# Spacing GpSimd's indirect gathers over the slots of two pairs, and building the tokens' places in two steps, in a masked attention kernel

## The chip, the cores and the metric

The kernel runs on one core of one Trainium2 chip. The metric is the device time of one execution in microseconds (us). The core has five engines that each work through a queue of their own in program order: TensorE (PE), VectorE (DVE), ScalarE (ACT), GpSimd (POOL) and SyncE (SP); they wait for each other through semaphores only. DMA transfers are issued from the queues of SP and POOL (and of ACT at the very end).

## The reference

`x` is (8, 512, 1024) f32: 8 batches, 512 features, 1024 tokens. The mask `cond` is (8, 1024) of zeros and ones.

```python
xt = transpose(x, (0, 2, 1))
q = xt @ Wq.T                                    # 512 -> 512, 8 heads of 64
qh = q.reshape(B, T, 8, 64).transpose(0, 2, 1, 3)
scores = einsum('bhqd,bhkd->bhqk', qh, qh) / 8   # q = k = v
logits = (scores * cmask + (1 - cmask) * -1e30) * rmask
ctx = einsum('bhqk,bhkd->bhqd', softmax(logits), qh)
out = x + transpose(ctx.reshape(B, T, 512) @ Wo.T, (0, 2, 1))
```

About half the tokens are kept (mask 1). All dropped tokens of a batch have one and the same result, that of the mean of the values, so only the kept tokens and one mean row need attention.

## The kernel before, in words

**Tiles and loops.** For each batch the kept tokens are gathered into NK = 544 rows: four chunks of 128 and a last one of 32 (NC = 5 chunks). The work is a sequence of 32 pairs of heads, p = 0 to 31, four in each batch: pair (b, pr) is batch b and heads 2 pr and 2 pr + 1. Each pair is walked in five slots c = 0 to 4, one for each chunk. In a slot PE makes the scores `s` (L601), ACT their exponentials `e` (L605; `el` for the last, short chunk), and VectorE adds up the slot before (`add_up`, L622, two instructions). After the five slots `attend` multiplies exponentials and values (`av`, PE L638) and ACT copies the sums to `cT` (L654).

**Side work in the slots.** Each slot also carries pieces of other pairs and batches: projections `pq` (PE L529, copied by ACT to `qT`, L536), values `v` (PE L551, ACT L554), the squared lengths of the values and their largest (`sq` ACT L559, `len` and `top` DVE L561 and L568), which `bias_of` turns round on PE (`top`, L574) and makes into the maximum `m` and the exponentials' bias (DVE L576 to L579); the reciprocal sums, turned on DVE (`rt`, L708), spread by DMA (`rb`) and multiplied in by `contexts` (DVE L726 to L735).

**Tokens in and out.** `turn` transposes the next batch's x on VectorE (L417) and SP stores it to DRAM as rows `xd`. `search` (DVE L473, L476) finds which token goes to which row (`source`), and `gather` (POOL indirect DMA, L485) fetches those rows as `xin`, five gathers a batch. `put_mean` and `collect` (PE L512, L498) transpose them to `xc`. `output` (PE L750, ACT L757) makes a batch's finished rows, which POOL stores to DRAM as `od` (L759). `fetch` (POOL indirect DMA, L852) gathers them back in the order of all 1024 tokens, eight gathers `g_0` to `g_7` a batch, by the indices `block_origin`. `finish_blocks` (DVE transpose L819 and add L822) adds each `g` to x, and SP stores the sum.

**The places.** `block_origin` comes from `place_all`, which runs once, in batch 0 at pair 1, slot 4: five VectorE instructions make `home` (L1048 to L1052), PE transposes it (`home_t`, L1054), and two more VectorE instructions copy it to `placed` and `origin` (L1055, L1056). `place_blocks` (DVE L803, 16 casts) makes `block_origin` from `placed` at pair 2, slot 2.

**What sets the order.** Everything is written in the order in which each engine is to run it; nothing reorders it. The tables in `late` name the slots (pr, c) of the side work: `TURN`, `SEARCH` (`LATER` for batch 0) and `FINISH`. In a slot the order is scores, `add_up` of the slot before, contexts, turn, search, gather, loads, fetch, places, finish, then projections, bias, outputs, collects and values.

Of the kernel before, what the change touches and what calls it, by code (L numbers as in the profile page):

```python
# [10 lines left out]
F32 = mybir.dt.float32  # L11
# [294 lines left out]
def attention_of_kept_tokens(ctx, tc, x, mask, wq, wo, out, ident, wqT, woT, verdict, flag):  # L306


    nc = tc.nc
    B, D, T = x.shape  # L310
    P = 128
# [3 lines left out]
    NT = T // P  # L315
# [5 lines left out]
    NC = -(-LONG // P)  # L321
    LAST = NC - 1
# [6 lines left out]
    def fit_to(n):  # L329
        nonlocal NK, KH, END  # L330
        NK, KH, END = n, n // 2, n - LP
        assert DK % END == 0
        sizes[:] = [P] * LAST + [END]
        places[:] = [slice(END + c * P, END + (c + 1) * P) for c in range(LAST)] + [slice(0, END)]

    sb = ctx.enter_context(tc.tile_pool(name="fsb", bufs=2))
# [11 lines left out]
    block_origin = keep.tile([P, B, NT], I32, name="block_origin")  # L348
# [6 lines left out]
    homes = [keep.tile([B * NT, P], F32, name=f"home_{i}") for i in range(2)]  # L355
# [3 lines left out]
    def bank(name):  # L359
        return ps.tile([P, NB], F32, tag="t", name=name, bufs=4)  # L360
# [119 lines left out]
    def gather(b, i):  # L480
        n = sizes[i]
        if i == 0:
            xins[b] = []
        xin = sb.tile([P, D], F32, tag="xin", name=f"xin_{b}_{i}", bufs=NC)
        nc.gpsimd.indirect_dma_start(  # L485
            out=xin[:n, :],
            out_offset=None,
            in_=xds[b],
            in_offset=bass.IndirectOffsetOnAxis(ap=searches[b][2][:n, i : i + 1], axis=0),
        )  # L490
        xins[b].append(xin)
# [246 lines left out]
    ods, gs, xrs = {}, {}, {}  # L738
# [107 lines left out]
            )  # L846
            gs[b, i] = g

    def fetch(b):
        for i in range(NT):  # L850
            g = sb.tile([P, D], F32, tag="g", name=f"g_{b}_{i}", bufs=NT)
            nc.gpsimd.indirect_dma_start(  # L852
                out=g,
                out_offset=None,
                in_=ods[b],
                in_offset=bass.IndirectOffsetOnAxis(
                    ap=block_origin[:, b, i : i + 1], axis=0
                ),
            )
            gs[b, i] = g  # L860

    def finish_tokens(b, i):

# [50 lines left out]
    def load_weights(w, nm, queue=None):  # L914
        ws = []
        for e in range(ND):
            t = sb.tile([P, D], F32, tag="g", name=f"{nm}_{e}", bufs=NT)
            (queue or nc.sync).dma_start(t, w[e * P : (e + 1) * P, :])
            ws.append(t)
        return ws  # L920
# [122 lines left out]
    def place_all():  # L1043

        BC = B * NT
        mrow, rank = seen["mrow"], seen["rank"]
        home, wrap = homes
        nc.vector.tensor_scalar(home, rank, float(-NK), None, ALU.add)  # L1048
        nc.vector.tensor_tensor(home, home, mrow, ALU.mult)
        nc.vector.tensor_scalar(home, home, float(NK - 1 + END), None, ALU.add)  # L1050
        nc.vector.tensor_scalar(wrap, home, float(NK), float(-NK), ALU.is_ge, ALU.mult)
        nc.vector.tensor_tensor(home, home, wrap, ALU.add)  # L1052
        pt = bank("home_t")
        nc.tensor.transpose(pt[:, :BC], home, ident[:BC, :BC])  # L1054
        nc.vector.tensor_copy(placed, pt[:, :BC].rearrange("p (b c) -> p b c", c=NT))  # L1055
        nc.vector.tensor_copy(origin, placed)  # L1056

    def late(n):
        fit_to(n)
        weights["wq"] = order_columns(load_weights(wq, "wq"), "wq")  # L1060
        mean_of(0)
        for i in range(NC):
            gather(0, i)
        queries_of(0)
        load_batch(1, nc.gpsimd)
        load_ranks(1, nc.gpsimd)
        put_mean(0)
        for i in range(NC):
            collect(0, i)
            if i < ND:  # L1070
                turn_weights(wqT, "wq", i)
        weights["wo"] = load_weights(wo, "wo", nc.gpsimd)
        for hf in range(2):
            project(pairs[0], hf)
        values(pairs[0])
        project(pairs[1], 0)
        bias_of(pairs[0])


        TURN = [(0, 2), (0, 4), (1, 0), (1, 1)]  # L1080
        SEARCH = {(1, 0): (0, 1), (1, 1): (2,), (1, 2): (3,), (1, 3): (4,)}
        LATER = {(1, 1): (0,), (1, 2): (1,), (1, 3): (2, 3), (1, 4): (4,)}

        FINISH = {
            (2, 3): (0,),
            (2, 4): (1, 2),
            (3, 0): (3,),
            (3, 1): (4,),
            (3, 2): (5,),
            (3, 3): (6,),  # L1090
            (0, 1): (7,),
        }
        FINISH_LAST = {(3, 1): (0, 1), (3, 2): (2, 3), (3, 3): (4,)}
        for p, pair in enumerate(pairs):
            b, pr = pair
            before = pairs[p - 1] if p else None
            todo = slots_of(p)
            for c in range(NC):
                scores(pair, c)
                if c:  # L1100
                    add_up(pair, c - 1)
                if c == 0 and before:
                    add_up(before, LAST)
                    if p + 1 < len(pairs):
                        invert(before)
                    else:
                        inv = inverses(before)
                if p + 1 == len(pairs):
                    if c == 1:
                        spread(before, inv)  # L1110
                        contexts(before)
                elif c == (4, 2, 3, 4)[pr] and before:
                    contexts(before)
                if (p, c) in ((2, 3), (len(pairs) - 2, 1)):
                    bias_of(pairs[p + 1])
                if b + 1 < B:
                    if (pr, c) in TURN:
                        turn(b + 1, TURN.index((pr, c)))
                    if pr < 2 and pr * NC + c < NN * ND:
                        add_features(b + 1, pr * NC + c)  # L1120
                    if pr == 1 and c == 3:
                        mean_of(b + 1)
                    for i in (SEARCH if b else LATER).get((pr, c), ()):
                        search(b + 1, i)
                    if pr == 0 and c == 1:
                        queries_of(b + 1)
                    if pr == 1 and c == (3 if b else LAST):
                        for i in range(NC):
                            gather(b + 1, i)
                if pr == 3 and c == 0 and b + 2 < B:  # L1130
                    load_batch(b + 2)
                    load_ranks(b + 2)
                if pr == 1 and c == 2 and b > 0:
                    load_rest(b - 1)
                if pr == 2 and c == 0 and b > 0:
                    fetch(b - 1)
                if p == 1 and c == 4:
                    place_all()
                if p == 2 and c == 2:
                    place_blocks()  # L1140
                for i in (FINISH if b + 1 < B or pr == 0 else FINISH_LAST).get((pr, c), ()):
                    of = b - 2 if pr == 0 else b - 1
                    if of in BLOCKS:
                        finish_blocks(of, i)
                for task in todo[c]:
                    task()
                issue_stores()
            if p + 1 < len(pairs):
                attend(pair)
        last = pairs[-1]  # L1150
        add_up(last, LAST)
        attend_last(last)
        for i in (0, LAST, *range(1, LAST)):
            end_output(B - 1, i)
        for i in range(5, NT):
            finish_blocks(B - 2, i)
        issue_stores()
        worst = sb.tile([P, 2], F32, tag="worst", name="worst")
        nc.vector.tensor_reduce(
            worst[:, 0:1], low.rearrange("p h c -> p (h c)"), axis=AX.X, op=ALU.min  # L1160
        )
        nc.vector.tensor_reduce(worst[:, 1:2], lowest, axis=AX.X, op=ALU.min)
        nc.vector.tensor_tensor(worst[:, 0:1], worst[:, 0:1], worst[:, 1:2], ALU.min)
        pt = bank("worst_t")
        nc.tensor.transpose(pt[:1, :P], worst[:, 0:1], ident)
        one = sb.tile([1, 1], F32, tag="one", name="one")
        nc.vector.tensor_reduce(one, pt[:1, :P], axis=AX.X, op=ALU.min)
        nc.vector.tensor_scalar(one, one, TINY, None, ALU.is_lt)
        nc.vector.tensor_copy(flag, one)
        issue_stores()  # L1170
        fetch_last(B - 1)
        for i in range(NT):
            finish_tokens(B - 1, i)
# [96 lines left out]
```

## Time and profile before

| | |
|---|---|
| median of 3 runs | 774.1 us (770.66, 774.1 and 782.16) |
| profiled execution | 778.75 us, of which the span is 776.8 us and 1.95 us lie around it |
| mean granted clock of TensorE | 0.929 |
| busy in the span | PE 668.4 us (86%), DVE 533.5 (69%), ACT 378.6 (49%), POOL 171.4 (22%) |
| mean DMA rate | 150 GB/s |

Rows of the trace are read so: start and duration in us, engine, line, operation, out<-in, shape and count; in brackets the engine's idle time just before the row and what ended it. A row with x8 is eight like instructions joined. `PEclk` is the TensorE clock that was granted, as a share of full speed. In the rows below, pairs and slots are found by their time: pair 1 of batch 0 ends its last scores at 65.56 us, and batches 1 to 6 take the stretches from 141.30 to 676.70 us.

### The profile page before, as it was taken

Reading aid. Unit: us, or ns where it says so; the run is one execution under the profiler, and the core shown is the slowest. Engines: PE = TensorE matmul, PEld = TensorE weight load, DVE = VectorE, ACT = ScalarE, POOL = GpSimd, SP = SyncE. Lnnn points to the kernel's source line nnn. Section 1 sums busy time; section 2 is a strip of 40 time slices with the busy share of each in tenths; the row PEclk is TensorE's granted clock in tenths of the full one; section 3 lists DMA queues with packets and bytes.
Section 4 is the critical chain, followed back from the end, with each engine's and each line's share of the span. In section 5 each row is a group of like instructions: output and inputs, shape, how many; then the busy total and the mean of one; then the engine's idle time right before and its main releaser. Section 6 shows DMA issues by size and latency. Waiting matters only on the chain.

```text
span 776.8 us, 11988 instructions
## 1 busy us (share of the span) xinstructions
PE 668.4 (86%) x4139; PEld 387.6 (50%) x4139; DVE 533.5 (69%) x1568; ACT 378.6 (49%) x763; POOL 171.4 (22%) x222
## 2 busy tenths in 40 slices
PE   5795899978999599995999989997999599997972
PEld 4663565445555265553555555554554265553431
DVE  6178758736877389863898579866887389545762
ACT  5384567334664256534474546646574256434400
POOL 4702000070102501044010521035001600033030
PEclk9797999988999799996999999999999789998985
DMA  7534042771479605894248834895468700753247
GB/s 273 193 111 128 18 154 61 187 209 37 153 180 224 196 3 172 209 230 141 84 136 213 213 111 153 208 230 163 153 166 211 222 4 22 181 137 113 54 129 210
DMA packets 96703, 116.41 MB, mean 150 GB/s; under 512 B 10304, under 2 KB 74304, under 8 KB 96624
## 3 DMA queue, kind: packets, MB, share of 16 engines
q1 hardware_dynamic: 79552, 74.07, 36.2%
q0 software_dynamic: 12848, 39.30, 15.8%
q10 hardware_dynamic: 4224, 2.10, 0.9%
q8 instruction: 36, 0.59, 0.3%
q14 instruction: 43, 0.35, 0.2%
HBM read 72.78 MB, written 42.65 MB: 149 GB/s over the span
## 4 chain that ended last, share of the span: by engine, by line
PE 79%; ACT 7%; DVE 5%; issue 3%; another core or an unknown queue 2%; DMA 2%; POOL 1%; DVEq 0%; POOLq 0%
PE s L601 20%; PE av L638 18%; PE pq L529 16%; PE po L750 13%; ACT e L605 5%; PE xc L498 3%; PE v L551 2%; PE pa L770 2%; DVE junk L622 1%; DVE junk L473 1%; DMA g<-od,origin 1%; PE xt L393 1%; PE po L786 1%; PE mean L512 1%
## 5 line engine op out<-in xcount | busy, mean ns | idle before, releaser
L622 DVE CUSTOM_DVE_ANT_0 junk<-e,valid 128x544 f32<-128x544 f32 x256 | 185.1, 723 | 97.8 <-ACT e L605 79.6
L601 PE MATMUL s<-qT 64*128 64x272 f32 (+1 forms) x1280 | 190.6, 438 | 56.6 <-ACT e L605 44.8
L605 ACT ACTIVATE e<-s,bias 128x544 f32<-128x544 f32 x256 | 170.8, 712 | 64.2 <-PE s L601 33.8
L601 PEld LDWEIGHTS s<-qT 64*128 64x128 f32 (+1 forms) x1280 | 95.8, 182 | 141.3 <-ACT e L605 77.0
L529 PE MATMUL pq<-xc,wqT 128*128 128x272 f32 x512 | 136.4, 410 | 4.7 <-issue 3.7
L638 PE MATMUL av<-e,v 128*64 128x272 f32 x1024 | 130.2, 401 | 0.4
L529 PEld LDWEIGHTS pq<-xc,wqT 128*128 128x128 f32 x512 | 93.7, 193 | 40.1 <-issue 11.2
L750 PE MATMUL po<-woT,cT 128*128 128x512 f32 (+1 forms) x448 | 107.4, 436 | 0.0
L638 PEld LDWEIGHTS av<-e,v 128*64 128x64 f32 x1024 | 69.6, 138 | 51.6 <-ACT v L554 8.8
L759 POOL DMA_DIRECT2D od<-oc x56 | 29.9, 536 | 273.4 <-ACT oc L757 272.4
L750 PEld LDWEIGHTS po<-woT,cT 128*128 128x128 f32 (+1 forms) x448 | 47.1, 150 | 52.5 <-issue 51.3
L654 ACT COPY cT<-av 128x272 f32<-128x272 f32 x62 | 21.4, 388 | 101.2 <-PE av L638 79.9
L852 POOL DMA_INDIRECT g<-od,block_origin x56 | 57.3, 1022 | 18.9 <-issue 15.5
L757 ACT COPY oc<-po 128x512 f32<-128x512 f32 (+1 forms) x35 | 18.3, 522 | 81.4 <-PE po L750 81.4
L536 ACT COPY qT<-pq 128x272 f32<-128x272 f32 x64 | 24.7, 386 | 60.4 <-PE pq L529 57.2
L381 POOL TENSOR_SCALAR valid<-count,kept 128x544 f32<-128x544 f32 x8 | 13.5, 1693 | 177.4 <-DVE sums L622 177.3
L485 POOL DMA_INDIRECT xin<-xd,source x40 | 41.1, 1028 | 48.2 <-DVE bias L579 26.7
L561 DVE TENSOR_REDUCE len<-sq 128x10 f32<-128x640 f32 x32 | 25.8, 808 | 30.1 <-ACT sq L559 30.1
L417 DVE STREAM_TRANSPOSE xt<-x 128x1024 f32<-128x1024 f32 x28 | 34.7, 1240 | 13.6 <-DMA xd<-xt 13.5
L473 DVE TENSOR_SCALAR_CACHE_REDUCE junk<-rank,key 128x1024 f32<-128x1024 f32 (+4 forms) x40 | 39.7, 993 | 1.6 <-ACT rank L1020 1.6
L822 DVE TENSOR_TENSOR xr<-o,xr 128x512 f32<-128x512 f32 x56 | 38.8, 692 | 1.9
L819 DVE STREAM_TRANSPOSE o<-g 128x512 f32<-128x512 f32 x56 | 39.2, 701 | 0.0
(139 smaller groups left out, 638.5 us busy)
## 6 DMA issues: line engine op xcount, KB each, us to landing
x<-in_x_dram SPq DMA_DIRECT2D x56, 256.0 KB
xd<-xt SPq DMA_DIRECT2D x112, 128.0 KB
xr<-in_x_dram SPq DMA_DIRECT2D x28, 512.0 KB
out_dram<-xr SPq DMA_DIRECT2D x24, 512.0 KB
rb<-row SPq DMA_DIRECT2D x60, 160.0 KB
od<-oc POOLq DMA_DIRECT2D x28, 256.0 KB
rank<-ranks SPq DMA_DIRECT2D x6, 512.0 KB
xd<-xt POOLq DMA_DIRECT2D x8, 256.0 KB
```

Source lines behind the costliest of these rows:

```text
L417: nc.vector.transpose(xt.rearrange("p k (d f) -> p k d f", d=ND), xs[b][r][:, :, at : at + n].rearrange("p d (k t) -> p k d t", t=Q),)
L473: nc.vector.tensor_scalar(junk[:, :n], rank[:, i * P :], key[:, col], 0.0, ALU.is_le, ALU.add, accum_out=found[:, col])
L485: nc.gpsimd.indirect_dma_start(out=xin[:n, :], out_offset=None, in_=xds[b], in_offset=bass.IndirectOffsetOnAxis(ap=searches[b][2][:n, i : ...
L529: nc.tensor.matmul(pq[:, :KH], wqT[:, d, pr * P : (pr + 1) * P], xcs[b][:, d, cols], start=(d == 0), stop=(d == ND - 1),)
L601: nc.tensor.matmul(s[to, h, :KH], qT[heads[h], keys], qT[heads[h], queries], start=True, stop=True)
L605: nc.scalar.activation(e[:, hf if c < LAST else 0, :, :], s[:, :, :KH], AF.Exp, bias=biases[pair][:, c : c + 1], scale=SCALE,)
L622: nc.vector.tensor_tensor_reduce(junk[:, :n].rearrange("p (f k) -> p f k", k=KH), e[:, :, h, :], (valid if c < LAST else part).rearrange(" ...
L638: nc.tensor.matmul(av[head, :KH], v[keys, c, head], e[keys, hf if c < LAST else 0, h, :], start=(c == 0), stop=(c == LAST),)
L750: nc.tensor.matmul(po[k * n : (k + 1) * n, :w], cTs[b, pr][:, i * P : i * P + n], woT[:, pr, k * w : (k + 1) * w], start=(pr == 0), stop=( ...
L819: nc.vector.transpose(o.rearrange("p k t -> p (k t)"), gs[b, i])
L822: nc.vector.tensor_tensor(to, o, to, ALU.add)
L852: nc.gpsimd.indirect_dma_start(out=g, out_offset=None, in_=ods[b], in_offset=bass.IndirectOffsetOnAxis(ap=block_origin[:, b, i : i + 1], a ...
```

## The change

`fetch` now issues one gather, and a table `FETCH` calls it once in each of the slots (2, 0) to (2, 4) and (3, 0) to (3, 2). Before, all eight were issued at (2, 0). The five gathers of the next batch's tokens go by the tables `GATHER` and `GATHER_LATER` (batch 0); before, all five stood at (1, 3), in batch 0 at (1, 4). `FINISH` has one block in each slot from (2, 3) to (3, 4); before, (2, 4) had two and (3, 4) none. `place_all` is cut in two: the five VectorE instructions for `home` move to pair 0, slot 1, and the transposition with its two copies, now `turn_places`, stays at pair 1, slot 4.

```diff
-    def fetch(b):
-        for i in range(NT):
-            g = sb.tile([P, D], F32, tag="g", name=f"g_{b}_{i}", bufs=NT)
-            nc.gpsimd.indirect_dma_start(
...
+    def fetch(b, i):
+        g = sb.tile([P, D], F32, tag="g", name=f"g_{b}_{i}", bufs=NT)
+        nc.gpsimd.indirect_dma_start(
...
         nc.vector.tensor_tensor(home, home, wrap, ALU.add)
+
+    def turn_places():
+        BC = B * NT
         pt = bank("home_t")
-        nc.tensor.transpose(pt[:, :BC], home, ident[:BC, :BC])
+        nc.tensor.transpose(pt[:, :BC], homes[0], ident[:BC, :BC])
         nc.vector.tensor_copy(placed, pt[:, :BC].rearrange("p (b c) -> p b c", c=NT))
         nc.vector.tensor_copy(origin, placed)
...
+        GATHER = {(1, 3): (0, 1), (1, 4): (2, 3), (2, 0): (4,)}
+        GATHER_LATER = {(1, 4): (0, 1, 2), (2, 0): (3,), (2, 1): (4,)}
+        FETCH = {(2, k): (k,) for k in range(NC)} | {(3, k): (NC + k,) for k in range(NT - NC)}
         FINISH = {
             (2, 3): (0,),
-            (2, 4): (1, 2),
-            (3, 0): (3,),
-            (3, 1): (4,),
-            (3, 2): (5,),
-            (3, 3): (6,),
+            (2, 4): (1,),
+            (3, 0): (2,),
+            (3, 1): (3,),
+            (3, 2): (4,),
+            (3, 3): (5,),
+            (3, 4): (6,),
             (0, 1): (7,),
         }
...
-                    if pr == 1 and c == (3 if b else LAST):
-                        for i in range(NC):
-                            gather(b + 1, i)
+                    for i in (GATHER if b else GATHER_LATER).get((pr, c), ()):
+                        gather(b + 1, i)
...
-                if pr == 2 and c == 0 and b > 0:
-                    fetch(b - 1)
+                if b > 0:
+                    for i in FETCH.get((pr, c), ()):
+                        fetch(b - 1, i)
+                if p == 0 and c == 1:
+                    place_all()
                 if p == 1 and c == 4:
-                    place_all()
+                    turn_places()
```

GpSimd's queue in batch 1, from the first gather of batch 2's tokens (`xin`) through the fetches of batch 0's rows (`g`). The number behind a tile's name counts the tiles in the order in which the program makes them.

```order
 L485 DMA xin_0_1575<-xd_1278,source_1062 128x512
 L485 DMA xin_1_1577<-xd_1278,source_1062 128x512
-L485 DMA xin_2_1579<-xd_1278,source_1062 128x512
-L485 DMA xin_3_1581<-xd_1278,source_1062 128x512
-L485 DMA xin_4_1583<-xd_1278,source_1062 32x512
-L852 DMA g_0_1666<-od_1428,block_origin 128x512
-L852 DMA g_1_1668<-od_1428,block_origin 128x512
-L852 DMA g_2_1670<-od_1428,block_origin 128x512
-L852 DMA g_3_1672<-od_1428,block_origin 128x512
-L852 DMA g_4_1674<-od_1428,block_origin 128x512
-L852 DMA g_5_1676<-od_1428,block_origin 128x512
-L852 DMA g_6_1678<-od_1428,block_origin 128x512
-L852 DMA g_7_1680<-od_1428,block_origin 128x512
+L485 DMA xin_2_1590<-xd_1278,source_1062 128x512
```

The same piece of the queue after the change:

```order
L485 DMA xin_2_1590<-xd_1278,source_1062 128x512
L485 DMA xin_3_1592<-xd_1278,source_1062 128x512
L485 DMA xin_4_1664<-xd_1278,source_1062 32x512
L851 DMA g_0_1666<-od_1428,block_origin 128x512
L851 DMA g_1_1681<-od_1428,block_origin 128x512
L851 DMA g_2_1703<-od_1428,block_origin 128x512
L851 DMA g_3_1742<-od_1428,block_origin 128x512
L851 DMA g_4_1784<-od_1428,block_origin 128x512
L851 DMA g_5_1880<-od_1428,block_origin 128x512
L851 DMA g_6_1905<-od_1428,block_origin 128x512
L851 DMA g_7_1923<-od_1428,block_origin 128x512
```

The thirteen gathers stand in the same order and directly behind each other, as before; only the counts show that they are issued at later points of the program's text.

VectorE's queue in batch 0 before the change, around pair 1, slot 4: the last search (L473, L476), the five instructions for `home`, and the copies from its transposition.

```order
L473 TENSOR_SCALAR junk_4_758,found_329<-rank_328,key 128x512
L476 TENSOR_SCALAR source_330<-found_329 128x1
L1048 TENSOR_SCALAR home_90<-rank_row 64x128
L1049 TENSOR_TENSOR home_90<-home_90,mrow 64x128
L1050 TENSOR_SCALAR home_90<-home_90 64x128
L1051 TENSOR_SCALAR home_91<-home_90 64x128
L1052 TENSOR_TENSOR home_90<-home_90,home_91 64x128
L1055 COPY placed<-home_t 128x64
```

After the change the five stand 70 rows further up, in pair 0, behind the first `add_up` and ahead of `len`; the search is followed by the copy `placed` at once.

```order
L622 ISA junk_0_0_1_475,sums_86<-e_0_0_445,valid_313 128x544
L622 ISA sums_86 128x1
L1045 TENSOR_SCALAR home_90<-rank_row 64x128
L1046 TENSOR_TENSOR home_90<-home_90,mrow 64x128
L1047 TENSOR_SCALAR home_90<-home_90 64x128
L1048 TENSOR_SCALAR home_91<-home_90 64x128
L1049 TENSOR_TENSOR home_90<-home_90,home_91 64x128
L561 TENSOR_REDUCE len_1_501<-sq_1_499 128x10
```

VectorE's queue at slot (3, 4) of batch 1 after the change: the contexts' last two instructions, the block that the change puts here, and `len` of the next values. Before, `len` followed the contexts at once, and this block stood one slot earlier.

```order
L734 TENSOR_TENSOR cT_2_1834<-cT_2_1834,rb_2_1863 128x544
L735 COPY cT_2_1834<-qT_2_1238 128x1
L819 STREAM_TRANSPOSE o_6_1975<-g_6_1905 128x512
L822 TENSOR_TENSOR xr_1505<-o_6_1975,xr_1505 128x16x32
L561 TENSOR_REDUCE len_1_1990<-sq_1_1988 128x10
```

One block more lies ahead of `len` at (3, 4), and one fewer at (2, 4); all other slots keep their number.

More of the change, by code (lines that the diff above doesn't have):

```diff
@@ L847, in fetch_last @@
             gs[b, i] = g
-    def fetch(b):
-        for i in range(NT):
-            g = sb.tile([P, D], F32, tag="g", name=f"g_{b}_{i}", bufs=NT)
[L852 to L860, printed above, removed]
+    def fetch(b, i):
+        g = sb.tile([P, D], F32, tag="g", name=f"g_{b}_{i}", bufs=NT)
+        nc.gpsimd.indirect_dma_start(
+            out=g,
+            out_offset=None,
+            in_=ods[b],
+            in_offset=bass.IndirectOffsetOnAxis(ap=block_origin[:, b, i : i + 1], axis=0),
+        )
+        gs[b, i] = g
     def finish_tokens(b, i):
```

## The prediction

> **What bounds the kernel.** I read the engines' shares first, then the chain that ended last, then batches side by side, then the longest waits.
>
> ```profile
> PE 668.4 (86%) x4139; PEld 387.6 (50%) x4139; DVE 533.5 (69%) x1568; ACT 378.6 (49%) x763; POOL 171.4 (22%) x222
> PE 79%; ACT 7%; DVE 5%; issue 3%; another core or an unknown queue 2%; DMA 2%; POOL 1%; DVEq 0%; POOLq 0%
> ```
>
> TensorE is busy 86% of the span and makes 79% of the chain. GpSimd is busy 22% and makes 1%. So work taken off GpSimd is worth nothing by itself; what counts is what PE waits for and at which clock it runs. The windows view over batches 1 to 6 (length; busy time of PE, its weight loads, DVE, ACT and POOL with instructions in brackets; granted clock; DMA share; GB/s):
>
> ```profile
> 141.30:233.10 91.80, 82.09 (x503) 47.45 (x501) 63.05 (x183) 45.69 (x95) 20.20 (x25) 0.93 0.57 159
> 233.10:325.30 92.20, 80.62 (x502) 46.02 (x500) 66.38 (x192) 46.04 (x95) 19.62 (x25) 0.93 0.58 159
> 325.30:417.80 92.50, 80.24 (x502) 45.81 (x500) 65.30 (x191) 45.82 (x95) 19.71 (x25) 0.93 0.57 159
> 417.80:502.10 84.30, 78.78 (x503) 44.83 (x501) 66.63 (x194) 45.91 (x95) 20.79 (x25) 0.98 0.63 174
> 502.10:585.20 83.10, 76.91 (x502) 44.02 (x500) 65.37 (x189) 46.03 (x95) 21.29 (x25) 1.00 0.65 177
> 585.20:676.70 91.50, 80.25 (x502) 45.91 (x500) 62.21 (x191) 42.47 (x83) 17.04 (x22) 0.93 0.47 126
> ```
>
> Six batches with the same program take two lengths: some 92.0 us four times and some 83.7 us (the mean of 84.30 and 83.10) twice. The 8.3 us between them lie around the gathers. GpSimd's row of thirteen, its first and last of each kind, with one stretch of 16.6 us over it in batch 1 and the same stretch in batch 5, and what ACT does in batch 1:
>
> ```profile
> 159.22 1.44 POOL L485 DMA_INDIRECT xin<-xd,source  x1 [0.43 <-DMA xr<-in_x_dram]
> 164.87 0.87 POOL L485 DMA_INDIRECT xin<-xd,source  x1 [0.31 <-issue]
> 166.05 0.95 POOL L852 DMA_INDIRECT g<-od,block_origin  x1 [0.30 <-issue]
> 175.06 1.14 POOL L852 DMA_INDIRECT g<-od,block_origin  x1 [0.30 <-issue]
> 163.40:180.00 16.60, 9.02 (x54) 5.68 (x52) 4.02 (x13) 5.45 (x10) 9.84 (x10) 0.75 0.59 188
> 524.00:540.60 16.60, 13.02 (x95) 8.27 (x87) 10.99 (x32) 9.89 (x17) 11.12 (x10) 1.00 0.57 177
> 178.08 1.32 ACT L605 ACTIVATE e<-s,bias 128x544 f32<-128x544 f32 x2 [6.39 <-remote]
> ```
>
> In a long batch PE is busy 9.02 of the 16.6 us at clock 0.75, against 13.02 at 1.00 in a short one, and ACT stands 6.39 us for something that the profile can't name. The same row of gathers lies in both, so it is a condition of the stall but doesn't decide it alone. The longest single wait that names its cause is in batch 0:
>
> ```profile
> PE home_t L1054 <- DVE home L1052: 8.8, 1, 8.8
> ```
>
> **Gathers and fetches: 0.** What ties an instruction of GpSimd to a slot is its place in GpSimd's own queue and the semaphores it waits for. The queue's order is the same after the change, row for row, and nothing that belongs to a slot stands between the gathers. What each gather waits for (its `source` column, the stored `xd` or `od` rows, the collect that frees its buffer) is the same too and is older than the first of them: in the rows above gather follows gather by 0.30 us of "issue". So I expect thirteen starts at the same distance, (175.06 - 159.22) / 12 = 1.32 us. SP's and ACT's queues keep their order as well. The bounds of this zero are the stalls: four long batches could become short, 4 x 8.3 = 33 us below, or two short ones long, 2 x 8.3 = 17 us above. I take 0, because I see nothing that changes them; a different draw of one batch is 8.3 us either way.
>
> **The places: about 10 us.** Batch 0, pair 1, slot 4, by the timeline of PE and VectorE and the windows:
>
> ```profile
> 64.87 0.69 PE L601 MATMUL s<-qT 64*64 64x272 f32 x8 [0.38 <-ACT e L605]
> 74.40 0.37 PE L1054 MATMUL home_t<-ident,home 64*128 64x64 f32 x1 [8.84 <-DVE home L1052]
> 75.95 5.60 PE L638 MATMUL av<-e,v 128*64 128x272 f32 x32
> 50.74 3.89 PE L638 MATMUL av<-e,v 128*64 128x272 f32 x32
> 82.10 1.19 PE L601 MATMUL s<-qT 64*128 64x272 f32 x8
> 72.92 0.21 DVE L1048 TENSOR_SCALAR home<-rank_row 64x128 f32<-64x128 f32 x1
> 74.06 0.28 DVE L1052 TENSOR_TENSOR home<-home,home 64x128 f32<-64x128 f32 x1
> 74.80 0.22 DVE L1055 COPY placed<-home_t 128x64 f32<-128x64 f32 x1 [0.46 <-PE home_t L1054]
> 77.41 0.82 DVE L561 TENSOR_REDUCE len<-sq 128x10 f32<-128x640 f32 x1 [2.15 <-ACT sq L559]
> 84.25 0.72 DVE L622 CUSTOM_DVE_ANT_0 junk<-e,valid 128x544 f32<-128x544 f32 x1 [3.87 <-ACT e L605]
> 93.91 0.28 DVE L576 TENSOR_REDUCE m<-top 128x1 f32<-128x128 f32 x1
> 94.34 2.07 PE L529 MATMUL pq<-xc,wqT 128*128 128x272 f32 x8 [1.03 <-DVE m L576]
> 97.36 2.97 PE L638 MATMUL av<-e,v 128*64 128x272 f32 x24
> 65.50:74.40 8.90, 0.06 (x5) 0.01 (x1) 8.35 (x30) 0.71 (x1) 4.94 (x5) 0.71 0.37 111
> 74.40:78.00 3.60, 3.60 (x16) 2.28 (x18) 1.01 (x3) 1.49 (x3) 0.24 (x1) 0.50 0.10 35
> 78.00:81.50 3.50, 3.50 (x29) 1.76 (x25) 2.18 (x13) 0.00 (x0) 0.00 (x0) 0.79 0.02 5
> ```
>
> PE ends its scores at 64.87 + 0.69 = 65.56 and stands until 74.40, since `home` is last in a full VectorE queue (busy 8.35 of 8.90 us). The clock is down to 0.50 afterwards, and `av` takes 5.60 us in place of the 3.89 of the pair before: 1.71 us more.
>
> After the change `home` is ready in pair 0 already (shown below), so `home_t` can run at 65.56. The values and `av` behind it in PE's queue wait for exponentials and copies of ACT alone, and with the 3.89 us `av` and its short chunk end near 72, in place of 82.10. That is 10 us for PE, but VectorE doesn't get faster by as much, and PE meets it again. VectorE loses four pieces: `home` itself, 72.92 to 74.34, is 1.42; the idle ahead of `placed` 0.46; ahead of `len` 2.15; ahead of the first `add_up` of pair 2 3.87. Together 7.90 us. From 84.25 to 93.91 it runs without a gap, so `m` moves from 93.91 to 86.01. Before, PE's second projection waited 1.03 us for `m` and `av` came 97.36 - 93.91 = 3.45 us behind `m`. By the new order of PSUM banks, only the last transposition of the values, just ahead of `av`, waits for that `m`; the projection no longer does. So `av` can start when `m` is over, 86.30, and some 0.3 for that transposition: 86.6 in place of 97.36, **10.8 us**. Behind it every engine's queue is the same and no later step hangs on a point of time, so this is carried to the end.
>
> From above, 10.8 is the limit set by VectorE. From below: PE is idle some 2.7 us ahead of that transposition, which could cost half the clock once more (1.71 us, as above), and two transfers have less time until they are used: the spread sums `rb` start 1.42 + 0.46 + 2.15 = 4.0 us earlier and are used 7.9 earlier, the gathered tokens `xin` start no earlier and are used 10 earlier. I leave 2 us for these. That makes 7 to 11, and I take 10, nearer the upper end, because the DMA share of the two rows from 74.40 on (0.10 and 0.02) shows that hardly anything is under way then.
>
> The page "TensorE: Matmul & The Clock Gate" of the Trainium skill, Part 1, says that the clock is halved after an idle window of about 3.4 us and is back after as long a busy one. The rows of 74.40 and 78.00 agree with it in kind. By that rule an idle time of 2.7 us need not halve the clock, and the gain would be 10.8; by the row of 5.60 us it would be 9.1.
>
> The five instructions themselves move to pair 0, slot 1:
>
> ```profile
> 41.77 0.08 DVE L622 DVE_READ_ACCUMULATOR2_ANT sums<- 128x1 f32 x1
> 45.00 0.82 DVE L561 TENSOR_REDUCE len<-sq 128x10 f32<-128x640 f32 x1 [3.15 <-ACT sq L559]
> ```
>
> VectorE is idle 3.15 us there, waiting for ACT; that hides 1.42. Without that cover the cost is 1.42 once.
>
> **The blocks of FINISH: 0.** The sum of VectorE's work in a batch stays. Slot (2, 4) loses one block, slot (3, 4) gets one, ahead of `len`:
>
> ```profile
> 189.55 0.70 DVE L819 STREAM_TRANSPOSE o<-g 128x512 f32<-128x512 f32 x1
> 190.28 0.69 DVE L822 TENSOR_TENSOR xr<-o,xr 128x512 f32<-128x512 f32 x1
> 209.75 0.15 DVE L735 COPY cT<-qT 128x1 f32<-128x1 f32 x1
> 218.71 0.23 DVE L579 TENSOR_SCALAR bias<-pens,m 128x5 f32<-128x5 f32 x1
> 226.16 1.32 ACT L605 ACTIVATE e<-s,bias 128x544 f32<-128x544 f32 x2
> 231.29 1.25 DVE L417 STREAM_TRANSPOSE xt<-x 128x1024 f32<-128x1024 f32 x1 [3.13 <-DMA xd<-xt]
> ```
>
> A block is 190.28 + 0.69 - 189.55 = 1.42 us. VectorE can lag by this from 209.82 on, through a stretch without gaps, until the idle 3.13 us ahead of 231.29 take the lag up. Queued behind the block are `len`, `top`, the sums and the next pair's bias; the bias is made at 218.71 + 0.23 = 218.94 and ACT first uses it at 226.16, 7.2 us later, so a lag of 1.42 reaches neither ACT nor PE. So 0. If that cover is gone it is 1.42 in each of batches 1 to 6, 8.5 us.
>
> **The sum.** 0 - 10 + 0 on the profiled execution's own 778.75 us gives 768.75. That execution is 4.65 us above the median of the runs, about half of a long batch's 8.3, so I carry the difference to the median: 774.1 - 10 = **764 us**.
>
> **Rivals.** First, that the gathers do spread, or that their stalls go for another reason, and the long batches become short: for it speaks that two of six batches show it; against it the unchanged queue. Two to four batches are 17 to 33 us on top of the 10: 731 to 747. I give it 0.12.
>
> Second, that batch 0 hides most of it: another semaphore ahead of `av` (a PSUM bank that `placed` must free) keeps PE behind VectorE's queue, and only `home` and the idle behind it go, 1.42 + 0.46 = 1.9 us: 772. For it speaks that VectorE is full there in any case; against it that I find no such wait in the new queue. 0.14.
>
> Third, on the other side: the block at (3, 4) makes PE wait at the next pair's exponentials in each of six batches, 1.42 us and half the clock behind it, 1.71, together 6 x 3.13 = 18.8, less the 10: 783. It decides from 10 / 6 = 1.7 us a batch. Against it stands the 3.13 us of idle in which VectorE gets back. 0.06.
>
> The forecast keeps 0.68. Within it the runs of before alone differ by 11.5 us, from 770.66 to 782.16, or one and a half long batches; I allow one batch each way, 756 to 772. With the second rival and the nearer part of the first the range is 746 to 776. A measurement of this kernel can tell about 2% from no change, that is 15.5 us: below 758.6 counts as faster, above 789.6 as slower. Faster: the first rival's 0.12, and a draw of one short batch more within the forecast, 0.08, together 0.20. Slower: 0.02, if the third rival comes with a long batch more. The rest, 0.78, is within.
>
> **What would show it.** The places: the wait of `home_t` for `home` is gone, PE's scores of pair 2 begin near 72 us, VectorE goes from the searches to `m` near 86 with hardly a gap, and `av` of pair 2 starts near 87; a batch 0 that is shorter by less than 5 us proves the second rival. The gathers: thirteen of them still 1.3 us apart in each batch, `xin` and `g` without a gap, and batches of some 92 or some 84 us; gathers one slot apart prove me wrong. FINISH: an idle time of VectorE ahead of `xt` in the next batch that is 1.4 us shorter, and no new wait of PE for `e` at the change of batch. The forecast fails if the number of long batches changes by two or more, since that is as large as the whole gain.

## The result, and the profile after

The changed kernel takes 745.84 us (median of 4 runs, 739.82 to 755.92) against 772.38 us before (4 runs), a ratio of 0.9632 with a 95% interval of 0.9527 to 0.9736. The forecast was 764 and its range reached down to 746: the kernel gained 26.5 us where 10 were forecast. A ratio leaves out every run more than 1.5% above the fastest of its kernel, so it is not quite the quotient of two medians. The comparisons further down ran on five chips; before took 773 to 781 us on three of them and 716 to 718 us on the other two, so a time is only set against before on the same chip.

The page of the changed kernel has a shorter span, more of it TensorE's, and the same work:

```profile
span 754.1 us, 11987 instructions
PE 665.9 (88%) x4139; PEld 387.3 (51%) x4139; DVE 531.8 (71%) x1568; ACT 377.9 (50%) x763; POOL 171.5 (23%) x222
PE 80%; DVE 6%; ACT 6%; issue 4%; DMA 2%; another core or an unknown queue 1%; POOL 1%; DVEq 0%; POOLq 0%
```

This profiled execution took 755.92 us, 10 more than the median, so of the 22.7 us by which its span is shorter I use only the places, not the sum. First batch 0, where the prediction put its 10 us, by the timelines of PE and VectorE:

```profile
66.22 0.27 PE L1054 MATMUL home_t<-ident,home 64*128 64x64 f32 x1
67.76 3.89 PE L638 MATMUL av<-e,v 128*64 128x272 f32 x32 [0.57 <-ACT v L554]
72.19 1.19 PE L601 MATMUL s<-qT 64*128 64x272 f32 x8
86.95 0.30 PE L551 MATMUL v<-ident,qT 128*128 128x128 f32 x1 [0.52 <-DVE m L576]
87.18 3.89 PE L638 MATMUL av<-e,v 128*64 128x272 f32 x32
73.65 0.21 DVE L1055 COPY placed<-home_t 128x64 f32<-128x64 f32 x1
74.01 0.81 DVE L561 TENSOR_REDUCE len<-sq 128x10 f32<-128x640 f32 x1
86.52 0.28 DVE L576 TENSOR_REDUCE m<-top 128x1 f32<-128x128 f32 x1
45.74 0.82 DVE L561 TENSOR_REDUCE len<-sq 128x10 f32<-128x640 f32 x1 [2.11 <-ACT sq L559]
```

`home_t` waits for nothing, `av` is back at 3.89 us, VectorE runs from the searches through `placed` and `len` to `m` without the idle times of before, and PE's last transposition of the values waits for `m`. Pair 2's `av` comes 87.18 - 66.22 = 20.96 us behind `home_t`; before, it came 97.36 - 65.56 = 31.80 us behind the point at which `home_t` could have started. The difference is 10.8 us. The idle time ahead of `len` in pair 0 is 2.11 where it was 3.15 (part of it hides the five instructions).

Then the batches. The windows run from 17.9 us ahead of one batch's first gather to the same point of the next, as in the prediction's rows, for batches 1 to 5; below them GpSimd's gathers 3 and 4 in batches 1, 2 and 4:

```profile
131.10:222.95 91.85, 82.69 (x503) 47.47 (x501) 61.48 (x182) 45.61 (x95) 20.19 (x25) 0.93 0.58 158
222.95:309.04 86.09, 80.08 (x503) 45.71 (x502) 66.80 (x192) 46.06 (x96) 20.62 (x25) 0.96 0.63 172
309.04:398.34 89.30, 79.00 (x500) 45.34 (x499) 64.16 (x189) 45.23 (x95) 19.14 (x25) 0.94 0.59 160
398.34:483.65 85.31, 78.61 (x503) 44.87 (x501) 66.58 (x191) 45.53 (x95) 20.96 (x25) 0.98 0.64 176
483.65:569.19 85.54, 78.35 (x502) 45.01 (x500) 64.98 (x191) 45.53 (x95) 20.21 (x25) 0.96 0.62 169
153.43 0.95 POOL L485 DMA_INDIRECT xin<-xd,source  x1 [0.31 <-issue]
246.79 0.94 POOL L485 DMA_INDIRECT xin<-xd,source  x1 [1.93 <-PE s L601]
423.08 1.28 POOL L485 DMA_INDIRECT xin<-xd,source  x1 [2.78 <-DMA od<-oc]
```

The thirteen gathers are still in one row; nothing is spread over slots. But where before had 92 us in batch 2, there are 86.09 now, and batch 2 has a pause of 1.93 us ahead of its fourth gather, which before had not. Batches 1 and 3 have no pause and are long. The wait for ACT's exponentials, PE's largest, has halved (before, then after, from the two views of waits):

```profile
PE s L601 <- ACT e L605: 44.8, 55, 5.6
```

```profile
PE s L601 <- ACT e L605: 22.6, 45, 2.2
```

So two things gained: batch 0, as forecast, and some of the long batches, which the prediction had put at 0.

### The profile page after: what moved, and what is told of

It is laid out like the page before. It is cut to its first block, busy times and chain, and to the rows that moved or that the text cites. A ratio compares the mean times of both kernels' runs of the same rounds, so it can differ in the third digit from the quotient of the medians.

```text
span 754.1 us, 11987 instructions
## 1 busy us (share of the span) xinstructions
PE 665.9 (88%) x4139; PEld 387.3 (51%) x4139; DVE 531.8 (71%) x1568; ACT 377.9 (50%) x763; POOL 171.5 (23%) x222
## 4 chain that ended last, share of the span: by engine, by line
PE 80%; DVE 6%; ACT 6%; issue 4%; DMA 2%; another core or an unknown queue 1%; POOL 1%; DVEq 0%; POOLq 0%
PE s L601 20%; PE av L638 19%; PE pq L529 16%; PE po L750 14%; ACT e L605 4%; PE xc L498 3%; PE v L551 3%; PE pa L770 2%; DVE junk L622 2%; DVE junk L473 1%; DMA g<-od,origin 1%; PE xt L393 1%; PE po L786 1%; PE top L574 1%
## 5 line engine op out<-in xcount | busy, mean ns | idle before, releaser
L601 PE MATMUL s<-qT 64*128 64x272 f32 (+1 forms) x1280 | 185.6, 430 | 35.2 <-ACT e L605 22.6
L601 PEld LDWEIGHTS s<-qT 64*128 64x128 f32 (+1 forms) x1280 | 93.7, 178 | 118.0 <-issue 54.3
L638 PE MATMUL av<-e,v 128*64 128x272 f32 x1024 | 132.6, 410 | 0.7 <-ACT v L554 0.6
L638 PEld LDWEIGHTS av<-e,v 128*64 128x64 f32 x1024 | 72.2, 142 | 51.9 <-issue 11.4
L473 DVE TENSOR_SCALAR_CACHE_REDUCE junk<-rank,key 128x1024 f32<-128x1024 f32 (+4 forms) x40 | 39.7, 993 | 2.3 <-ACT rank L1017 2.2
```

The costliest lines, as they stand in the source:

```text
L473: nc.vector.tensor_scalar(junk[:, :n], rank[:, i * P :], key[:, col], 0.0, ALU.is_le, ALU.add, accum_out=found[:, col])
L601: nc.tensor.matmul(s[to, h, :KH], qT[heads[h], keys], qT[heads[h], queries], start=True, stop=True)
L638: nc.tensor.matmul(av[head, :KH], v[keys, c, head], e[keys, hf if c < LAST else 0, h, :], start=(c == 0), stop=(c == LAST),)
```

## The experiments

**The change taken apart.** Four kernels on one chip, beside before with 781.16 us. `place` has only the hunks on `place_all` and `turn_places`, `finish` only the table `FINISH`, `tables` only the new `fetch`, `GATHER`, `GATHER_LATER` and `FETCH`, and `place_finish` the first two without the third.

> Only the places are built in two steps (home in pair 0, slot 1; the transposition at pair 1, slot 4); gathers, fetches and FINISH as before. Theory D (the prediction's mechanism for batch 0, with the number of long batches left to chance): 772 - 10 = 762 us, the wait for home gone, and long batches of 92 us about as often as before (four of six in the profile of before). Rival P (the split also ends the long batches, by shifting the engines against the gathers): about 746, with mostly batches of 84 to 86 us.

> Only FINISH has one block a slot; places, gathers and fetches as before. Theory D: no change, 772 us. Rival F (the shifted blocks, and the PSUM banks that follow from them, end the long batches): 772 - 16 = 756 us, with the wait of 8.8 us for home still there.

> Only the calls of gather and fetch are spread over slots by the tables; places and FINISH as before. Theory D: the queues and waits of all engines are those of before, so no change, 772 us, thirteen gathers in a row. Rival G (spreading the calls does reach the chip in some way that the order of the queues doesn't show): 772 - 16 = 756 us.

> Places in two steps and FINISH one block a slot, but all gathers and fetches called in one place as before. Theory D and rivals P and F: the queues and waits are those of the changed kernel, so its time, about 746 us. Rival G: 746 + 16 = 762 us.

| kernel | median us | ratio to before, 95% interval |
|---|---|---|
| place | 760.71 | 0.9819 (0.9705 to 0.9932) |
| finish | 759.65 | 0.9674 (0.9482 to 0.9867) |
| tables | 779.62 | 1.0042 (0.9977 to 1.0108) |
| place_finish | 743.96 | 0.9550 (0.9431 to 0.9669) |

The tables do nothing, and the change without them has its full gain: rival G falls. The places alone give 14 us with an interval of 5 to 23, which holds the 10.8 of the trace, and their profile has two short batches among batches 1 to 5, as before's has, so rival P falls. The time from batch 0's first gather to batch 1's is sharper: 91.99 us in before and in `finish` and 92.38 in `tables`, but 81.05 to 81.29 in the four profiles with the new places (`place`, `place_finish` and the changed kernel's two), 11 us less. FINISH alone gives 25 us with an interval of 10 to 40, with `home` where it was. That ratio rests on two of its six runs, but all six (745.68 to 764.18) lie below the lowest of before's 17 (767.99). Theory D's zero for it falls, rival F stands.

What FINISH does is read in its batches 2 and 4 (windows) and in GpSimd's third and fourth gather of batch 2:

```profile
231.84:317.31 85.47, 78.94 (x503) 45.03 (x502) 66.83 (x192) 46.21 (x96) 21.20 (x25) 0.98 0.63 174
409.45:488.65 79.20, 76.66 (x503) 44.15 (x501) 65.94 (x191) 45.31 (x95) 21.68 (x25) 1.00 0.68 188
252.71 1.05 POOL L485 DMA_INDIRECT xin<-xd,source  x1 [0.30 <-issue]
255.86 0.94 POOL L485 DMA_INDIRECT xin<-xd,source  x1 [2.10 <-PE s L601]
```

Both have the pause (2.07 us in batch 4). In the seven profiles of before, of the changed kernel (two) and of these four kernels, on chips where before takes 772 us or more, that holds in each of the 35 batches whose length can be read (batches 1 to 5; the pause is the longest idle time ahead of the fourth or fifth gather, the length runs to the next batch's first gather):

```
pause ahead of gather 4 or 5   batches   length us, mean (lowest to highest)
0.97 us or more                19        84.0 (79.2 to 88.1)
0.47 us or less                16        91.3 (89.3 to 93.9)
batches 1 to 6 with a pause: before 2, tables 2, place 2; finish 4, changed kernel 4 and 4, place_finish 5
```

The two groups don't overlap. Batch 1 never has the pause and batch 5 always has it; batch 2 has it in all four profiles with the new FINISH and in none of the three without. FINISH adds 2.25 paused batches on average (17 / 4 against 6 / 3), and 2.25 x 7.3 us is 16 us, which is what the change gained beyond batch 0 (26.5 - 10.8 = 15.7).

**Why FINISH makes a pause.** As I read it, the fourth gather has to wait for the landing of an earlier store `od`. The row of 423.08 above names it (2.78 us); most other rows with a pause name PE's scores, so for them this is inferred. The rows of batch 2 in before, of PE's first output and SP's issue of `xr` (the transposition ahead of the stores is the prediction's row of 231.29), and then all three with FINISH alone:

```profile
228.44 3.60 PE L750 MATMUL po<-woT,cT 128*128 128x512 f32 x8
240.11 3.05 SPq L814 DMA_DIRECT2D xr<-in_x_dram  x4
```

```profile
227.18 3.60 PE L750 MATMUL po<-woT,cT 128*128 128x512 f32 x8
241.15 3.39 SPq L814 DMA_DIRECT2D xr<-in_x_dram  x4
231.80 1.25 DVE L417 STREAM_TRANSPOSE xt<-x 128x1024 f32<-128x1024 f32 x1 [3.26 <-DMA xd<-xt]
```

Against PE's outputs, `xt` now stands at 231.80 - 227.18 = 4.62 us, where it stood at 231.29 - 228.44 = 2.85, and the 2 MB load of `xr` at 13.97 us, where it stood at 11.67: 2.3 us later. That the stores `od`, which GpSimd issues by PE's and ACT's progress, then land later beside `xr` is argued, not shown. The experiment for this link delays `xr` in the kernel before through one number that ACT writes into its tile. In the expectations that follow, theory S is that a long row of gathers without a pause makes the stalls; rival C is that the bytes moved do, and rival V that FINISH shortens the batches by what it does on VectorE and PE, the pause only going with it (in the expectation of `pause` this last one is called rival C).

```diff
+        if b + 2 < B:
+            nc.scalar.copy(xr[0:1, 0, 0:1], es[(b + 1, 1), 2][0:1, 1, 0, 0:1])
         for a in range(A):
             nc.sync.dma_start(xr[a * Q : (a + 1) * Q, :, :], in_blocks(x[b])[a])
```

> The kernel before, with a one-number copy on ACT into the tile xr at pair 1, slot 2 of batches 1 to 6, so that the 2 MB load of xr starts some 2.5 us later against PE, as it does in the kernel with FINISH alone. Theory S with its chain (xr later, so the stores od land later, so the fourth gather waits some 2 us and the row is cut): about as with FINISH alone, 16 to 20 us less than before, with a gap ahead of the fourth gather in most batches. Rival C: same as before.

> The kernel before with the load of xr some 2.5 us later against PE in batches 1 to 6, once more. Theory S with its chain: where before runs in about 780 us, 755 to 765, with gaps ahead of the fourth gather; where before runs in 717, the same as before. Rival V: where before runs in about 780 us, the same as before.

> The kernel before with the load of xr some 2.5 us later against PE, where before runs in about 775 us, if it does so this time. Theory S with its chain: gaps of 1 to 2 us ahead of the fourth gather and 750 to 765. Rival V: the same as before.

All three fell on the two chips on which before takes 716 to 718 us: ratios 1.0002 (0.9981 to 1.0023), 1.0020 (1.0003 to 1.0036) and 1.0000 (0.9978 to 1.0023). The half of the link that can be seen there holds. In batch 1, SP's issue of `xr` went from 146.57 in the profile of before to 151.29, which against PE's first output (136.69 and 136.76) is 4.65 us later, twice what FINISH does in batch 2. The fourth gather, which had no pause in any kernel without that delay or a copy on GpSimd, got one:

```profile
151.29 1.91 SPq L816 DMA_DIRECT2D xr<-in_x_dram  x4
164.66 0.95 POOL L485 DMA_INDIRECT xin<-xd,source  x1 [1.27 <-PE s L601]
```

That a later `xr` shortens the batches on the other three chips was not seen, so this link of the chain is not shown.

**A pause by hand, and a real spread.** `pause` is before with a copy on GpSimd, ahead of the fourth gather, that has to wait for ACT's exponentials of pair 2, slot 0. `spread` is the changed kernel with such a copy ahead of every slot's gathers in batches 1 to 7. The core of both:

```diff
+    def tie(pair, c):
+        b, pr = pair
+        t = sb.tile([1, 1], F32, tag="tie", name=f"tie_{b}_{pr}_{c}", bufs=1)
+        hf = 1 if c < LAST else 0
+        nc.gpsimd.tensor_copy(t, es[pair, c][0:1, hf, 0, 0:1])
```

> The kernel before, with one difference in batches 1 to 6: ahead of the fourth gather of tokens, GpSimd copies one number of the exponentials of pair 2, slot 0 (an instruction that has to wait for ACT), so that the row of thirteen gathers gets a pause of some 2 us behind its third. Theory S (a row of more than four or five gathers without a pause slows the semaphores between PE, ACT and DVE, and a pause of 2 us cuts the row to 3 and 10): batches of 84 to 86 us in place of 92, in all about 16 to 25 us less than before, though places and FINISH are those of before. Rival C (the pause only accompanies short batches; FINISH shortens them by what it does on VectorE): same time as before, batches of 92 us.

> The changed kernel, with a copy of one number of the slot's exponentials on GpSimd ahead of each slot's gathers and fetches in batches 1 to 7, so that they really run one or two a slot. Theory S: the stalls go altogether, batches of 80 to 83 us and clock 1.00, about 735 us or less. Rival C: the bytes and not the row count; the stalls stay at the size of the changed kernel or move, 745 us or more.

> The gathers really one or two a slot, once more. Theory S (a long row of gathers makes the stalls): where before runs in about 780 us, batches of 80 to 83 us and 705 to 730 us; where it runs in about 717, as the changed kernel, 706. Rival C (the stalls come with the bytes, not with the row): where before runs in 780 us, 745 or more.

> The kernel before with a pause of some 3 us behind the third gather of batches 1 to 6, once more. Theory S with its chain (a pause cuts the row, and less of it is left to stall in): where before runs in about 780 us, 755 to 765, as with FINISH alone; where before runs in 717, 725. Rival V (FINISH shortens the batches by what it does on VectorE and PE, the pause only goes with it): where before runs in about 780 us, 780 or a little more.

> The kernel before with a pause of some 3 us behind the third gather, where before runs in about 780 us, if it does so this time. Theory S with its chain: 755 to 765. Rival V: 780 or a little more.

| run | before on that chip, us | median us | ratio, 95% interval |
|---|---|---|---|
| pause | 717.14 | 725.13 | 1.0106 (1.0077 to 1.0134) |
| pause_again | 716.02 | 723.29 | 1.0102 (1.0075 to 1.0129) |
| pause_third | 773.43 (752.37 to 784.59) | 729.84 (729.06 to 732.92) | none |
| spread | 717.14 | 706.12 | 0.9852 (0.9829 to 0.9875) |
| spread_again | 781.05 | 708.07 | 0.9135 (0.9074 to 0.9196) |

Where before takes 773 us, the pause alone, with places and FINISH as before, is 44 us below the median of before and 22.5 below its fastest run (752.37), and every run of it is faster than every run of before: rival V, which had 780 or more, falls. Theory S fares better but missed too: it had 755 to 765. Windows of batches 1 and 2 of `pause_third`, and of batch 2 the copy, the fourth, fifth and last gather:

```profile
140.40:220.50 80.10, 76.76 (x503) 44.16 (x501) 62.96 (x183) 45.48 (x95) 22.50 (x26) 1.00 0.66 181
220.50:303.00 82.50, 77.27 (x503) 44.30 (x502) 67.22 (x194) 45.70 (x96) 22.09 (x26) 1.00 0.64 178
244.94 0.73 POOL L866 COPY tie<-e 1x1 f32<-1x1 f32 x1 [2.55 <-ACT e L605]
245.83 1.40 POOL L485 DMA_INDIRECT xin<-xd,source  x1 [0.16 <-PE s L601]
247.54 1.26 POOL L485 DMA_INDIRECT xin<-xd,source  x1 [0.30 <-PE s L601]
258.46 0.95 POOL L852 DMA_INDIRECT g<-od,block_origin  x1 [0.30 <-issue]
```

Behind the copy ten gathers run in one row, as long as the rows that follow FINISH's pause, and yet the batches take 80 to 83 us at clock 1.00, not the 84 to 86 that theory S gave a row cut to 3 and 10. So the length of the unbroken row can't be the whole condition. That the pause moves the ten gathers some 3 us later beside the other engines' work may count as well: `plain_sp` below shortens the row without moving it, but no run moves it without breaking it. Where before takes 717, the same pause costs 7 to 8 us. The real spread takes 706 and 708 us on the two kinds of chip; on the second it is 73 us below before and, beside the changed kernel's 753.64 on the same chip, 46 below that. Rival C falls. Windows of batches 1 and 2 of `spread_again`, and then some of GpSimd's rows of its batch 1:

```profile
130.50:211.00 80.50, 76.39 (x501) 44.16 (x501) 61.70 (x182) 45.27 (x95) 25.63 (x35) 1.00 0.65 179
211.00:290.40 79.40, 76.67 (x501) 44.14 (x501) 65.79 (x192) 45.25 (x95) 24.08 (x35) 1.00 0.66 185
155.99 0.67 POOL L863 COPY tie<-e 1x1 f32<-1x1 f32 x1 [2.47 <-ACT e L605]
165.46 0.26 POOL L863 COPY tie<-el 1x1 f32<-1x1 f32 x1 [1.30 <-ACT el L605]
174.32 0.67 POOL L863 COPY tie<-e 1x1 f32<-1x1 f32 x1 [7.03 <-ACT e L605]
```

Clock 1.00 and 79 to 81 us in each batch; the copies do wait (2.47, 1.30, 7.03 us), which is what makes one gather follow its slot. This is the version that beats both kernels.

**Gathers or bytes.** `plain_sp` is before with the eight fetches as plain loads of the same size, issued by SP, and `plain_pool` the same issued by GpSimd. Both leave out the order of the tokens.

```diff
-            nc.gpsimd.indirect_dma_start(
...
+            at = min(i * P, NK - P)
+            nc.sync.dma_start(g, ods[b][at : at + P, :])
```

> The kernel before, but the eight fetches of a batch are plain loads of 128 rows in a row from od, issued by SP; the order of all tokens is left out, the bytes are the same. Theory S: only five gathers in a row are left on GpSimd, so no long stall, batches of 80 to 84 us, 20 to 35 us less than before. Rival C: the bytes moved beside PE's work make the stall, so it stays: within 8 us of before.

> The kernel before with the eight fetches as plain loads by SP, once more; the order of all tokens is left out, the bytes are the same. Theory S: where before runs in about 780 us, 715 to 735, since only five gathers in a row are left. Rival C (bytes): 770 or more. Where before runs in 717: 715.

> The kernel before with the eight fetches as plain loads by SP (the order of all tokens is left out), where before runs in about 780 us, if it does so this time. Theory S: 715 to 735. Rival C (bytes): 770 or more.

> The kernel before with the eight fetches as plain loads of 128 rows in a row, issued by GpSimd itself in the same place of its queue; the order of all tokens is left out, the bytes and the queue are the same. Where before runs in about 775 us: theory S in the form that indirect gathers make the stalls, 715 to 735; in the form that any row of GpSimd's transfers does, 760 or more. Where before runs in 717, 715.

On the chips with 716 to 718 us `plain_sp` gives 0.9968 (0.9951 to 0.9984) and 0.9983 (0.9970 to 0.9997), that is 1 to 2 us. Where before takes 773.43 it takes 724.32 us (722.50 to 725.53), 49 below that median and 28 below before's fastest run, with the same bytes: rival C falls again. Windows of its batches 1 and 2 there:

```profile
140.30:222.60 82.30, 78.08 (x502) 44.96 (x500) 62.55 (x183) 45.83 (x95) 12.19 (x17) 0.98 0.64 178
222.60:302.00 79.40, 76.91 (x503) 44.06 (x501) 67.02 (x194) 45.33 (x95) 12.05 (x17) 1.00 0.66 185
```

This run takes eight transfers out of GpSimd's queue and makes them plain at once, so it doesn't tell which of the two counts. `plain_pool`, which would, fell on a chip with 717.87 us and took 725.41 there (1.012, 1.0054 to 1.0187), where 715 was expected; whether plain loads in GpSimd's queue would stall was not seen.

**The same kernels where nothing stalls.**

> The changed kernel once more, beside before, since before itself ran in 781 us beside the first experiments and in 717 us beside the second ones. Theory P2 (only the places gain time by themselves; FINISH gains only where the gathers' stalls exist, by making fewer of them): where before runs in about 717 us and has batches of 79 to 80 us, 717 - 11 = 706 us; where before runs in about 780, 745 to 755. Rival F2 (FINISH gains some 16 us by itself, with or without stalls): 26 us below before in either case, 691 where before has 717.

> FINISH alone once more. Theory S with its chain and rival V: where before runs in about 780 us, 760. Where before runs in 717: theory S 717, since there are no stalls; rival F2 (FINISH gains by itself) 700.

`after_again` fell on a chip where before takes 781.05: 753.64 us, 0.9676 (0.9587 to 0.9766), the first result once more. `finish_again` fell where before takes 716.02: 716.02 us, 0.9999 (0.9984 to 1.0013). FINISH gains nothing by itself; F2 falls. There, even thirteen gathers without a pause leave a batch short: its batch 1 has the fourth gather 0.30 us behind the third and this window:

```profile
141.20:220.20 79.00, 76.55 (x503) 44.30 (x501) 61.77 (x182) 45.41 (x95) 21.36 (x25) 1.00 0.66 183
163.50 0.95 POOL L485 DMA_INDIRECT xin<-xd,source  x1 [0.30 <-PE av L638]
```

So the row of gathers is one condition of the stalls and the chip another; by the ten gathers of `pause_third`, what runs beside the row may be a third. Where nothing stalls, `spread` still gains 11.0 us (706.12 against 717.14): the places' size.

## Why the prediction was right or wrong, point by point

**Places: right.** 7 to 11 was forecast and 10 taken; the trace gives 10.8, the upper end worked out from VectorE. `m` came at 86.52 with `home_t` 0.66 later than forecast, so 85.86 against 86.01 in the prediction's clock; `av` of pair 2 at 86.5 against 86.6. The two allowances were not needed: the transfers came in time, and PE stood 0.52 us ahead of its last transposition, not the 2.7 for which half a clock (1.71) was allowed, so what 2.7 us of idle time would have done was not seen.

**Gathers and fetches: the queue read right, its zero right for this part.** The queue kept its order, and `tables` shows that the part of the change that its words begin with does nothing. But "gather follows gather by 0.30 us" was read in batch 1 alone and didn't hold in batches 4 and 5 of the same profile, as shown below.

**FINISH: wrong, and this is the step that failed.** It was costed 0 because VectorE's lag of 1.42 us would be taken up in the idle 3.13 us ahead of `xt`. That idle time is a wait for a store that VectorE itself set off one step earlier, so it moved along: it is 3.26 us with FINISH alone. The lag went on to `xr`, 2.3 us later in batch 2. Neither 8.5 us of loss nor 0 came of it but a gain, 25 us (10 to 40) with FINISH alone where the gathers stall and nothing (0.9999) where they don't, and with it a pause ahead of gather 4 or 5 in 17 of 24 batches in place of 6 of 18. That the shifted `xr` makes this pause is argued; that a pause there takes the stalls away is shown by `pause_third`.

**The draw of long batches: wrong in kind.** The prediction saw six batches of one program in two lengths, took it for chance and called a different draw of one batch 8.3 us either way. In the rows of before, the two short batches already had idle times of 0.97 and 2.24 us ahead of gathers 4 and 5, and the four long ones had 0.30 or 0.31:

```profile
440.77 0.96 POOL L485 DMA_INDIRECT xin<-xd,source  x1 [0.97 <-PE av L638]
527.48 0.87 POOL L485 DMA_INDIRECT xin<-xd,source  x1 [2.24 <-issue]
```

The prediction quoted gathers of a long batch only and so didn't see it. The batches are no like draws: in seven profiles a batch is short exactly where GpSimd has this wait, and which batches have it changes with FINISH. The first rival, with 0.12, named the outcome (stalls that go for another reason, 17 to 33 us on top) and had its size nearly right: 16. The prediction had also named two long batches fewer as the sign that it fails.

**The second and third rival** did not come: `home` is gone from PE's path whole, and PE's wait for `e` fell from 44.8 to 22.6 us.

## What to carry to other kernels

When equal stretches of a program take two lengths, set the waits of every engine in a long one beside those in a short one before calling it chance, those of an engine with 22% busy time too. Moving DMA issues to other places of the program's text doesn't space them on an engine that isn't late; a small instruction that waits for the slot's own result does, and on a chip where the gathers stall it took the changed kernel from 753.64 to 708.07 us, where the text alone was worth nothing. And an idle time absorbs a lag only if what ends it doesn't depend on the lagging engine.

## What the runs showed of the hardware that was not expected

On some chips hand-offs between the other engines come late while GpSimd issues its row of indirect gathers, and they mostly stop doing so when the row is spread, interrupted or cut to five (708, 730 and 724 us, each where before takes 773 to 781). In batch 2 of before, ACT's second copy of `av` waits only for PE, whose last `av` ends at 255.47 by the trace, but begins at 258.37; later an exponential stands 3.54 us and VectorE 6.38 us for something without a name:

```profile
254.78 0.69 PE L638 MATMUL av<-el,v 64*64 64x272 f32 x8
258.37 0.39 ACT L654 COPY cT<-av 128x272 f32<-128x272 f32 x1 [1.75 <-remote]
265.79 0.71 ACT L605 ACTIVATE e<-s,bias 128x544 f32<-128x544 f32 x1 [3.54 <-remote]
270.16 0.17 DVE L515 TENSOR_SCALAR xc<-mean 128x4 f32<-128x4 f32 x1 [6.38 <-remote]
```

Beside the chips with 717 us, before loses some 56 to 64 us on the three others (773 and 781), with the same program on one core. What in the row does it, why ten gathers behind a pause don't, and why on some chips only, stays open. So does whether the delay of `xr` is the whole of FINISH's effect.
